# A scrap iota on GpSimd behind every second gather of a sorted graph-attention kernel

## The chip, the cores and the metric

The kernel runs on one core of one Trainium2 chip. The metric is the device time of one execution in microseconds (us), as the median of the runs shown. Durations inside the kernel come from one further execution that the hardware profiler recorded.

## The reference, cut to what matters

One layer of graph attention over 12,500 nodes of 64 features and 400,000 edges of 64 features. The edges come sorted by destination. Cut to what is computed:

```
h_src, h_dst = x[src], x[dst]
e     = leaky_relu(concat(h_src, h_dst, edge) @ W_attn + b_attn)      # one number per edge
alpha = softmax of e over the edges with the same dst
z     = segment_sum(alpha * (concat(h_src, edge) @ W_ne), dst)
out   = layernorm(x + relu(concat(x, z) @ W_out))
```

## The kernel before

**Tiling.** 512 consecutive edges are a group: 128 partitions by 4 places. There are 782 groups. The first 88 are worked off by one-hot matrix products, woven into the rest, and need no gather. The other 694 are the main part. They go in 45 batches, 41 of them of 16 groups and four smaller ones at the end; a batch is cut into tiles of up to four groups.

**Gathers.** For each group and place, GpSimd (POOL in the profile) issues one indirect DMA that fetches the source nodes' rows of 128 edges into a tile `zx` (`gather`, line 303; the DMA is line 314). A full tile takes 16 gathers, a batch of 16 groups takes 64. The first batch ("plain", 64 gathers) reads `x`. The later ones read `table`, in DRAM, in which each row of `x` has its score in front: 2,712 gathers. `zx` comes from the pool `feats` with eight buffers (`ZB = 8`), so gathers run up to two batches ahead of the products that read them, and a gather into a buffer waits until the products of the tile that held it before are done.

```
zx = feats.tile([P, SG, T, EW + D], F32, name="zx")
for g in range(n):
    for t in range(T):
        ...
        nc.gpsimd.indirect_dma_start(out=..., in_=table[:, :], in_offset=...)
```

**What a batch does.** `scores` copies the edges' features into `zx` on ScalarE (ACT, line 346) and makes the scores on VectorE (DVE, lines 348 to 366; line 355 is the first that needs the gathered rows). `softmax` runs over the whole batch in five stages that go from DVE to ACT to TensorE (PE) and back, with the work on the first 88 groups woven between the stages. Then `weights` (line 761), and `products` (line 775): 16 matmuls a tile, which read `zx` last and so set its buffer free. The products of a batch's first two tiles follow its softmax at once (`NOW = 2`). Those of the other two are put into `later`, and are done between the stages of the next batch's softmax. `add_in` (line 792) adds the products into the running sums `acc`; a block of nodes whose sums are complete is finished and written out.

**Order.** PE, DVE, ACT and SP run in the order in which the main loop is written (`manual_schedule`). GpSimd is not in that list: in the main loop its instructions are put in order by the framework's scheduler, which goes by its own estimate of times. Edge features, index lists and other plain loads are DMAs issued by SP.

**Front.** Ahead of the main loop, a front part loads `x`, makes the two scores of each node, writes `table`, and fetches windows of destination scores by seven indirect DMAs (`window`). It is written out by hand for all engines, POOL too. Behind it come a transpose, three small matmuls and three copies (lines 926 to 936) that make two products of the weights, `both` and `edge_both`, for which the scheduler finds a place.

Of the kernel before, what the change touches and what calls it, by code (L numbers as in the profile page):

```python
# [9 lines left out]
F32 = mybir.dt.float32  # L10
I32 = mybir.dt.int32
# [4 lines left out]
P = 128  # L16
# [13 lines left out]
SG = 4  # L30
# [18 lines left out]
NBC = 4  # L49
LATE = 8.0  # L50
NOW = 2

BF16 = mybir.dt.bfloat16
I16 = mybir.dt.int16
# [3 lines left out]
def sorted_path(ctx, tc, x, dst, idx, edge, w_ne, w_attn, b_attn, w_out, out, flag):  # L58
# [6 lines left out]
    nc = tc.nc  # L65
    N, D = x.shape
# [4 lines left out]
    NG = idx.shape[0]  # L71
# [5 lines left out]
    const = ctx.enter_context(tc.tile_pool(name="const", bufs=1))  # L77
# [3 lines left out]
    ident = const.tile([P, P], F32, name="ident")  # L81
# [51 lines left out]
    for i in range(2):  # L133
        nc.vector.memset(d3s[i], N)
    nc.vector.memset(mrow, FLOOR)
    nc.vector.memset(srow, 0.0)
    b_col = const.tile([P, 1], F32, name="b_col")
    wne = const.tile([P, D], F32, name="wne")
    wout = const.tile([D, 2, D], F32, name="wout")
    acc = const.tile([P, RING + S], F32, name="acc")  # L140
    xall = const.tile([P, NB, EW], F32, name="xall")

# [13 lines left out]
    both = const.tile([P, D], F32, name="both")  # L156
    twice = const.tile([P, P], F32, name="twice")
# [5 lines left out]
                   allow_small_or_imprecise_dtypes=True)  # L163
    places = const.tile([P, NB * NOD], I16, name="places")
    nc.gpsimd.iota(places, pattern=[[1, NB * NOD]], base=0, channel_multiplier=0,
                   allow_small_or_imprecise_dtypes=True)
# [16 lines left out]
    nc.vector.tensor_reduce(own, ident.rearrange("p (h n) -> p h n", n=ND), axis=AX.X, op=OP.add)  # L183
    node = const.tile([P, ND], F32, name="node")
    nc.vector.tensor_reduce(node, ident.rearrange("p (h n) -> p n h", n=ND), axis=AX.X, op=OP.add)
    meet = const.tile([1, 2], I32, name="meet")
    of_next = const.tile([1, 4], F32, name="of_next")
    scrap_row = const.tile([1, 1], F32, name="scrap_row")

    loop = ExitStack()  # L190
    chunks = loop.enter_context(tc.tile_pool(name="chunks", bufs=2))
# [115 lines left out]
    def gather(g0, n, srcs, b0, plain):  # L307
# [4 lines that stand above are left out]
                r = RP if g0 + g == NG - 1 else P  # L312
                at = srcs[0:r, g0 + g - b0, t:t + 1]
                nc.gpsimd.indirect_dma_start(  # L314
                    out=zx[0:r, g, t, 1:EW] if plain else zx[0:r, g, t, 0:EW], out_offset=None,
                    in_=x[:, :] if plain else table[:, :],
                    in_offset=bass.IndirectOffsetOnAxis(ap=at, axis=0))
        return zx

    fetched, early = {}, {}  # L320
# [479 lines left out]
                   allow_small_or_imprecise_dtypes=True)  # L800
    attn = pre.tile([P, 3 * D], F32, name="attn", bufs=1)
    nc.scalar.dma_start(out=attn, in_=w_attn.rearrange("k o -> o k").to_broadcast([P, 3 * D]))
    nc.scalar.dma_start(out=b_col, in_=b_attn.unsqueeze(0).to_broadcast([P, 1]))
    nc.scalar.dma_start(out=wne, in_=w_ne)
    nc.scalar.dma_start(out=wout, in_=w_out.rearrange("(h k) o -> k h o", h=2))
    lists = {0: listed(0)}
    xts = []
    for c0 in range(0, NB, CB):
# [15 lines left out]
    nc.sync.dma_start(out=meet, in_=dst[DG * GE - 1:DG * GE + 1].unsqueeze(0))  # L824
    sd = pre.tile([P, NB], F32, name="sd", bufs=1)
    NW = len(wins)
    d0p = const.tile([P, NW], I32, name="d0p")
    wks = [counts.rearrange("p h n -> p (h n)")[:, k * S:(k + 1) * S] for k in range(NW)]
    nc.scalar.activation(w_dst, attn[:, D:2 * D], AF.Copy)
    nc.scalar.activation(w_src, attn[:, 0:D], AF.Copy)  # L830
# [3 lines left out]
    with before:  # L834
# [23 lines left out]
        with tc.manual_schedule(engines={EngineType.DVE, EngineType.Pool, EngineType.Activation, EngineType.PE, EngineType.SP}):  # L858
            lots0 = [(g0, SG) for g0 in range(DG, DG + sizes[0], SG)]
            ahead = [gather(g0, n, lists[0], DG, True) for g0, n in lots0[:2]]  # L860
            for c0 in range(0, NB, CB):
                dots(c0, min(c0 + CB, NB), w_dst, sd[:, c0:min(c0 + CB, NB)])
            nc.vector.tensor_scalar(sd, sd, b_col, None, op0=OP.add)
            psd = psum.tile([P, SG, P], F32, name="pg", bufs=4)[0:NB, 0, :]
            nc.tensor.transpose(psd, sd, ident)
            sdt = pre.tile([NB, P], F32, name="sdt", bufs=1)
            nc.vector.tensor_copy(sdt, psd)
            nc.scalar.dma_start(out=sdflat[0:NB * P].rearrange("(b p) -> b p", p=P), in_=sdt)
            neighbours(0)
            for g0, n in lots0[:3]:  # L870
                early[g0] = edges(g0, n)
            for c0 in range(0, NB, 2 * CB):
                c1 = min(c0 + 2 * CB, NB)
                dots(c0, c1, w_src, xall[:, c0:c1, 0])
                nc.sync.dma_start(
                    out=table[c0 * P:c1 * P, :].rearrange("(b p) f -> p b f", p=P),
                    in_=xall[:, c0:c1, :])
            d0f = pre.tile([1, NG], F32, name="d0f", bufs=1)
            nc.vector.tensor_copy(d0f, d0i)
            for g0 in range(0, NG, 3 * P):  # L880
                n = min(3 * P, NG - g0)
                pb = psum.tile([P, SG, P], F32, name="pg", bufs=4).rearrange("p k n -> p (k n)")
                nc.tensor.matmul(pb[:, :n], ones_row, d0f[:, g0:g0 + n], start=True, stop=True)
                nc.scalar.activation(d0b[:, g0:g0 + n], pb[:, :n], AF.Copy)
            nc.vector.tensor_scalar(dn, d0f[:, 0:DG + 1], float(DN - 1), None, op0=OP.min)
            relf = pre.tile([1, DG], F32, name="relf", bufs=1)
            at = 0
            for n, many in CHUNKS:
                chunked = [a.rearrange("o (c g) -> o c g", g=n) for a in (relf[:, at:at + n * many], d0f[:, at:at + n * many])]
                nc.vector.tensor_tensor(chunked[0], chunked[1], chunked[1][:, :, 0:1].to_broadcast([1, many, n]), op=OP.subtract)  # L890
                at += n * many
            room = pre.tile([1, DG], F32, name="room", bufs=1)
            for a, b in spans:
                nc.vector.memset(room[:, a:b], float(ND - nodes_of(a)))
            over_ = pre.tile([1, DG], F32, name="over_", bufs=1)
            nc.vector.tensor_tensor(over_, relf, room, op=OP.subtract)
            nc.vector.tensor_reduce(fars[0:1, NK + len(spans):NK + len(spans) + 1], over_, axis=AX.X, op=OP.max)
            nc.vector.tensor_tensor(relf, relf, room, op=OP.min)
            nc.vector.tensor_scalar(rel, relf, 0.0, None, op0=OP.max)
            nc.vector.tensor_scalar(d0i, d0i, RING - 1, None, op0=OP.bitwise_and)  # L900
            window(0)
            ahead += [gather(g0, n, lists[0], DG, True) for g0, n in lots0[2:]]
            for k in range(1, NW):
                window(k)
            nc.scalar.activation(s_src, xall[:, :, 0], AF.Copy)
            nc.scalar.activation(count_, places[:, 0:P], AF.Copy)
            parted_row = pre.tile([DG, P, T], I32, name="parted_row", bufs=1)
            nc.vector.tensor_scalar(parted_row, ids[:, :, 0:T], P - 1, None, op0=OP.bitwise_and)
            low_row = pre.tile([DG, P, T], BF16, name="low_row", bufs=1)
            nc.scalar.activation(low_row, parted_row, AF.Copy)  # L910
            nc.sync.dma_start(out=low_rows, in_=low_row)
            of_dense = dense_list()
            dense_places(of_dense, fit)
            nc.vector.tensor_copy(of_next[:, 2:4], meet)
            nc.vector.tensor_tensor(of_next[:, 2:3], of_next[:, 2:3], of_next[:, 3:4], op=OP.is_equal)
            for c, (a, b) in enumerate(((starts[1], DG), (DG, begins[-2]))):
                nc.vector.tensor_tensor(earlies[:, NK + c:NK + c + 1], d0b[:, a:a + 1], d0b[:, b:b + 1], op=OP.subtract)
                nc.vector.tensor_scalar(earlies[:, NK + c:NK + c + 1], earlies[:, NK + c:NK + c + 1], -0.5, None, op0=OP.add)
            nc.vector.tensor_scalar(earlies[:, NK + 2:NK + 3], d0b[:, DG:DG + 1], -1.0, float(DN - 1), op0=OP.mult, op1=OP.add)
# [2 lines left out]
    rows = loop.enter_context(tc.tile_pool(name="rows", bufs=1))  # L922
    with tc.issue_after(last_of_front):
        nc.vector.memset(acc, 0.0)

    pwt = psum.tile([P, SG, P], F32, name="pg", bufs=4)
    nc.tensor.transpose(pwt[0:D, 0, :], wne, ident)
    for h in range(2):
        nc.scalar.dma_start(out=twice[h * D:(h + 1) * D, h * D:(h + 1) * D], in_=w_out[0:D, :])
    wt = work.tile([P, NBC // 2, P], F32, name="xtt", bufs=2)[0:D]  # L930
    nc.vector.tensor_copy(wt[:, 0, :], pwt[0:D, 0, :])
    nc.tensor.matmul(pwt[:, 1, 0:D], wt[:, 0, :], wout[:, 1, :], start=True, stop=True)
    nc.vector.tensor_copy(both, pwt[:, 1, 0:D])
    for g in range(2):
        nc.tensor.matmul(pwt[g * D:(g + 1) * D, 2, 0:D], wt[:, 0, D:P], wout[:, 1, :], start=True, stop=True)
    nc.vector.tensor_copy(edge_both, pwt[:, 2, 0:D])

    def late_of(k):

# [113 lines left out]
    k = 0  # L1053
# [703 lines left out]
```

## Time and profile before

| | before |
|---|---|
| median of 3 runs | 4319.42 us (4318.68 to 4326.91) |
| the profiled execution: time, span | 4329.98 us, 4328.3 us |
| granted TensorE clock, mean | 0.627 |
| busy: POOL, PE, DVE, ACT | 2637.9, 2048.5, 2000.6, 1048.5 us |
| gathers from `table` | 2712 of 947 ns |
| first and last start of these | 100.5 us, 4267.0 us |

Busy time is the time in which an engine works on some instruction; issuing instructions, semaphores and waits do not count. A row of a group reads: line, engine, operation, tiles, count, then busy time, mean duration in ns, idle time of that engine just before these instructions, and what ended most of that idle time ("issue" where the profile shows nothing that was waited for). A row of the timeline reads: start, duration, engine, line, operation, and in brackets the idle time before it with what ended it.

### The profile page before, as it was taken

Reading aid. Unit: us, or ns where it says so; the run is one execution under the profiler, and the core shown is the slowest. Engines: PE = TensorE matmul, PEld = TensorE weight load, DVE = VectorE, ACT = ScalarE, POOL = GpSimd, SP = SyncE. Lnnn points to the kernel's source line nnn. Section 1 sums busy time; section 2 is a strip of 40 time slices with the busy share of each in tenths; the row PEclk is TensorE's granted clock in tenths of the full one; section 3 lists DMA queues with packets and bytes.
Section 4 is the critical chain, followed back from the end, with each engine's and each line's share of the span. In section 5 each row is a group of like instructions: output and inputs, shape, how many; then the busy total and the mean of one; then the engine's idle time right before and its main releaser. Section 6 shows DMA issues by size and latency. Waiting matters only on the chain. (4 is left out here: it accounts for less than half of the span.)

```text
span 4328.3 us, 33932 instructions
## 1 busy us (share of the span) xinstructions
PE 2048.5 (47%) x8733; PEld 1795.4 (41%) x8733; DVE 2000.6 (46%) x5102; ACT 1048.5 (24%) x2333; POOL 2637.9 (61%) x2800
## 2 busy tenths in 40 slices
PE   0143334444554554554555455456455555443443
PEld 0143334444544444444444445444344433343433
DVE  4433434544445545444444445455444444444545
ACT  0111113222222323222223322233222223111112
POOL 6666666666666666656556565655555656666662
PEclk9999996555555555555565555556556555555555
DMA  9322223332322323232222222222222212322221
GB/s 115 63 58 51 53 59 66 61 65 47 66 56 56 69 51 76 50 68 56 56 55 57 57 57 56 52 61 64 37 51 47 60 36 51 71 37 47 53 55 27
DMA packets 490797, 246.18 MB, mean 57 GB/s; under 512 B 326795, under 2 KB 446154, under 8 KB 490594
## 3 DMA queue, kind: packets, MB, share of 16 engines
q1 hardware_dynamic: 398334, 150.93, 15.0%
q0 software_dynamic: 89056, 92.60, 13.9%
q8 instruction: 72, 1.18, 0.1%
q14 instruction: 131, 1.07, 0.1%
q10 hardware_dynamic: 3204, 0.39, 0.1%
HBM read 236.93 MB, written 6.75 MB: 56 GB/s over the span
## 5 line engine op out<-in xcount | busy, mean ns | idle before, releaser
L314 POOL DMA_INDIRECT zx<-table,srcs x2712 | 2568.2, 947 | 1599.5 <-issue 1199.5
L775 PE MATMUL pg<-w,zx 128*128 128x20 f32 (+9 forms) x5408 | 1113.9, 366 | 772.5 <-issue 689.6
L775 PEld LDWEIGHTS pg<-w,zx 128*128 128x128 f32 x5408 | 1140.3, 314 | 760.3 <-issue 686.6
L462 PE MATMUL pg<-big,lows 128*128 128x490 f32 (+3 forms) x704 | 398.3, 739 | 360.4 <-DVE lows L457 155.3
L462 PEld LDWEIGHTS pg<-big,lows 128*128 128x128 f32 x704 | 210.1, 315 | 495.1 <-issue 319.9
L568 PE MATMUL lines<-ident,bnd 128*1 128x128 f32 x180 | 52.8, 394 | 715.4 <-issue 487.1
L348 DVE TENSOR_TENSOR pr<-ze,fixed 128x1024 f32<-128x1024 f32 (+2 forms) x180 | 212.5, 1180 | 288.5 <-ACT fixed L345 164.6
L479 DVE TENSOR_TENSOR counts<-counts,pg 128x490 f32 (+3 forms) x88 | 48.0, 545 | 600.5 <-remote 461.9
L568 PEld LDWEIGHTS lines<-ident,bnd 128*1 128x1 f32 x180 | 12.1, 92 | 739.9 <-issue 502.3
L792 DVE TENSOR_TENSOR acc<-acc,pg 128x16 f32 (+9 forms) x694 | 128.5, 185 | 278.3 <-PE pg L775 147.5
L454 ACT ACTIVATE big<-places,place 128x490 f32<-128x490 int16 (+3 forms) x352 | 205.5, 584 | 205.5 <-remote 197.4
L350 DVE TENSOR_REDUCE fixed<-pr 128x16 f32<-128x1024 f32 (+2 forms) x180 | 214.1, 1189 | 24.8 <-DVE pr L348 10.1
L537 PE MATMUL pg<-xall,counts 128*128 128x256 f32 (+1 forms) x350 | 127.2, 490 | 161.6 <-issue 160.5
L415 PE MATMUL pg<-s_src,big 128*128 128x98 f32 x704 | 188.7, 446 | 1.3 <-issue 1.3
L346 ACT ACTIVATE zx<-ze 128x1024 f32<-128x1024 f32 (+2 forms) x180 | 185.2, 1029 | 8.7 <-issue 1.8
L345 ACT ACTIVATE fixed<-wrow 128x80 f32<-128x80 f32 (+9 forms) x180 | 47.0, 261 | 564.8 <-issue 289.7
L455 ACT ACTIVATE big<-big 128x490 f32<-128x490 f32 (+3 forms) x352 | 178.1, 506 | 11.2
L442 DVE TENSOR_TENSOR pr<-pr,pg 128x392 f32<-128x392 f32 x88 | 49.5, 563 | 278.6 <-remote 152.1
L415 PEld LDWEIGHTS pg<-s_src,big 128*128 128x128 f32 x704 | 172.8, 330 | 5.4 <-issue 5.2
L575 ACT ACTIVATE line<-tops 1x256 f32<-1x256 f32 x45 | 29.6, 658 | 575.3 <-DVE tops L677 424.4
L537 PEld LDWEIGHTS pg<-xall,counts 128*128 128x128 f32 (+1 forms) x350 | 84.4, 246 | 202.2 <-issue 191.7
L357 DVE TENSOR_TENSOR hot<-fixed,drel 128x320 bf16<-128x320 f32 (+9 forms) x180 | 112.1, 623 | 36.9 <-DVE fixed L355 22.8
(278 smaller groups left out, 2331.8 us busy)
## 6 DMA issues: line engine op xcount, KB each, us to landing
ze<-in_edge_dram SPq DMA_DIRECT2D x164, 512.0 KB
zx<-table,srcs POOLq DMA_INDIRECT x2712
low_of<-low_rows SPq DMA_DIRECT2D x88, 128.0 KB
ep<-in_edge_dram SPq DMA_DIRECT2D x88, 128.0 KB
ed<-in_edge_dram SPq DMA_DIRECT2D x29, 384.0 KB
table<-xall SPq DMA_DIRECT2D x7, 455.0 KB
ze<-in_edge_dram SPq DMA_DIRECT2D x8, 384.0 KB
out_dram<-yo SPq DMA_DIRECT2D x23, 128.0 KB
```

The costliest lines, as they stand in the source:

```text
L314: nc.gpsimd.indirect_dma_start(out=zx[0:r, g, t, 1:EW] if plain else zx[0:r, g, t, 0:EW], out_offset=None, in_=x[:, :] if plain else table ...
L346: nc.scalar.activation(zx[0:r, 0:n, :, EW:EW + D], ze[0:r, 0:n], AF.Copy)
L348: nc.vector.tensor_tensor(pr[0:r, 0:n], ze[0:r, 0:n], w_edge[0:r].unsqueeze(1).to_broadcast([r, n, T, D]), op=OP.mult)
L350: nc.vector.tensor_reduce(ysum[0:r, 0:n], pr[0:r, 0:n], axis=AX.X, op=OP.add)
L357: nc.vector.tensor_tensor(hot[0:r, 0:n], slots[0:r, 0:Sk].unsqueeze(1).unsqueeze(1).to_broadcast([r, n, T, Sk]), drel[0:r, :, b:b + n].rea ...
L415: nc.tensor.matmul(found[:, t, :], hot[:, :, t], s_src, start=True, stop=True)
L454: nc.scalar.activation(hi, places[:, 0:wide], AF.Square, bias=place[:, t, g:g + 1])
L455: nc.scalar.activation(hi, hi, AF.Relu, scale=-1.0, bias=1.0)
L462: nc.tensor.matmul(to, lows[t], highs[t], start=(t == 0), stop=(t == T - 1))
L537: nc.tensor.matmul(pairs[0:m * ND, 0:m * D], counts[:, h0:h0 + m, :].rearrange("l h n -> l (h n)"), xall[:, h0:h0 + m, 1:EW], start=(h0 == ...
L775: nc.tensor.matmul(pg[:, g, :], zx[:, g, t, 1:EW + D], w[:, g, t, :], start=(t == 0), stop=(t == T - 1))
L792: nc.vector.tensor_tensor(ag, ag, pg[:, g, :], op=OP.add)
```

## The change

Behind the gather of every second place (`t` odd) GpSimd gets an iota that writes a scrap tile of 128 x 300 numbers in 16 bits, `paused`, which nothing reads. This holds for gathers from `table` in all groups but the last: 677 groups with two iotas each, 1,354 iotas. The scrap tile needs room, so some small tiles (`b_col`, `wne`, `wout`, `meet`, `d0p`) move to a pool that the front part gives back, and the weight products `both` and `edge_both` are made inside the front, with their DMAs ahead of it.

```diff
+PAUSE = 300
...
+    paused = const.tile([P, PAUSE], I16, name="paused")
...
                     in_offset=bass.IndirectOffsetOnAxis(ap=at, axis=0))
+                if not plain and t % 2 and g0 + g + 1 < NG:
+                    nc.gpsimd.iota(paused, pattern=[[1, PAUSE]], base=0, channel_multiplier=0,
+                                   allow_small_or_imprecise_dtypes=True)
...
+    wout = pre.tile([D, D], F32, name="wout", bufs=1)
+    nc.scalar.dma_start(out=wout, in_=w_out[D:2 * D, :])
+    for h in range(2):
+        nc.scalar.dma_start(out=twice[h * D:(h + 1) * D, h * D:(h + 1) * D], in_=w_out[0:D, :])
...
(in the front, between the writing of the table and d0f:)
+            pwt = psum.tile([P, SG, P], F32, name="pg", bufs=4)
+            nc.tensor.transpose(pwt[0:D, 0, :], wne, ident)
+            wt = pre.tile([D, P], F32, name="wt", bufs=1)
+            nc.vector.tensor_copy(wt, pwt[0:D, 0, :])
+            nc.tensor.matmul(pwt[:, 1, 0:D], wt, wout, start=True, stop=True)
+            nc.vector.tensor_copy(both, pwt[:, 1, 0:D])
...
(the same steps, and the DMAs of twice, go out behind the front)
```

**Where the iotas stand in the built program.** The scheduler does not keep an iota behind its gather: an iota waits for nothing but the iota before it, on the one tile that they all write, while a gather waits for its buffer. In the built program the 1,354 iotas stand on POOL's queue in 45 lots, two of them (13 and 20) ahead of the first gather from `table`, all others within the first 1,184 gathers from it. The remaining 1,528 gathers have none. A stretch of POOL's queue, with the semaphore that each instruction waits for left out except on the iotas:

```
gathers x32
Iota paused 128x300 [each waits for the iota before]  x50      ahead of gather 480
gathers x16
Iota paused 128x300                                   x1       ahead of gather 496
gathers x16
Iota paused 128x300                                   x22      ahead of gather 512
gathers x32
Iota paused 128x300                                   x50      ahead of gather 544
...
Iota paused 128x300                                   x66      ahead of gather 1184
gathers x1528
```

Gathers are counted from 0 at the first one from `table`. Lots of one or two iotas, as the one ahead of gather 496, occur eleven times. Between gathers 96 and 288 the gathers stand in three runs of 64 with one lot between two runs.

More of the change, by code (lines that the diff above doesn't have):

```diff
@@ L136, in sorted_path @@
     nc.vector.memset(srow, 0.0)
-    b_col = const.tile([P, 1], F32, name="b_col")
-    wne = const.tile([P, D], F32, name="wne")
-    wout = const.tile([D, 2, D], F32, name="wout")
     acc = const.tile([P, RING + S], F32, name="acc")
@@ L185, in sorted_path @@
     nc.vector.tensor_reduce(node, ident.rearrange("p (h n) -> p n h", n=ND), axis=AX.X, op=OP.add)
-    meet = const.tile([1, 2], I32, name="meet")
     of_next = const.tile([1, 4], F32, name="of_next")
     scrap_row = const.tile([1, 1], F32, name="scrap_row")
+    paused = const.tile([P, PAUSE], I16, name="paused")
     loop = ExitStack()
@@ L802, in sorted_path @@
     nc.scalar.dma_start(out=attn, in_=w_attn.rearrange("k o -> o k").to_broadcast([P, 3 * D]))
+    b_col = pre.tile([P, 1], F32, name="b_col", bufs=1)
+    wne = pre.tile([P, D], F32, name="wne", bufs=1)
+    wout = pre.tile([D, D], F32, name="wout", bufs=1)
+    meet = pre.tile([1, 2], I32, name="meet", bufs=1)
     nc.scalar.dma_start(out=b_col, in_=b_attn.unsqueeze(0).to_broadcast([P, 1]))
     nc.scalar.dma_start(out=wne, in_=w_ne)
-    nc.scalar.dma_start(out=wout, in_=w_out.rearrange("(h k) o -> k h o", h=2))
+    nc.scalar.dma_start(out=wout, in_=w_out[D:2 * D, :])
+    for h in range(2):
+        nc.scalar.dma_start(out=twice[h * D:(h + 1) * D, h * D:(h + 1) * D], in_=w_out[0:D, :])
     lists = {0: listed(0)}
@@ L826, in sorted_path @@
     NW = len(wins)
-    d0p = const.tile([P, NW], I32, name="d0p")
+    d0p = pre.tile([P, NW], I32, name="d0p", bufs=1)
     wks = [counts.rearrange("p h n -> p (h n)")[:, k * S:(k + 1) * S] for k in range(NW)]
@@ L877, in sorted_path @@
                     in_=xall[:, c0:c1, :])
+            pwt = psum.tile([P, SG, P], F32, name="pg", bufs=4)
[4 more added lines that the diff above has]
+            nc.vector.tensor_copy(both, pwt[:, 1, 0:D])
+            for g in range(2):
+                nc.tensor.matmul(pwt[g * D:(g + 1) * D, 2, 0:D], wt[:, D:P], wout, start=True, stop=True)
+            nc.vector.tensor_copy(edge_both, pwt[:, 2, 0:D])
             d0f = pre.tile([1, NG], F32, name="d0f", bufs=1)
@@ L924, in sorted_path @@
         nc.vector.memset(acc, 0.0)
[L926 to L936, printed above, removed]
     def late_of(k):
```

## The prediction

> **What bounds the kernel now.** I read the page first, for the busy shares and the costliest groups.
>
> ```profile
> span 4328.3 us, 33932 instructions
> PE 2048.5 (47%) x8733; PEld 1795.4 (41%) x8733; DVE 2000.6 (46%) x5102; ACT 1048.5 (24%) x2333; POOL 2637.9 (61%) x2800
> L314 POOL DMA_INDIRECT zx<-table,srcs x2712 | 2568.2, 947 | 1599.5 <-issue 1199.5
> ```
>
> No engine is busy throughout; POOL is the busiest, nearly all of it gathers. Its idle time is of two kinds, which the timeline of POOL separates. These are the starts of the gathers around a few places: the first two from `table`, three tile borders, and the last gather that has iotas ahead of it in the new order.
>
> ```profile
> 100.52 0.95 POOL L314 DMA_INDIRECT zx<-table,srcs  x1 [0.30 <-issue]
> 101.77 0.94 POOL L314 DMA_INDIRECT zx<-table,srcs  x1 [0.30 <-issue]
> ...
> 282.36 0.94 POOL L314 DMA_INDIRECT zx<-table,srcs  x1 [0.30 <-issue]
> 290.06 0.95 POOL L314 DMA_INDIRECT zx<-table,srcs  x1 [6.76 <-issue]
> ...
> 820.05 0.95 POOL L314 DMA_INDIRECT zx<-table,srcs  x1 [0.30 <-issue]
> 824.78 0.95 POOL L314 DMA_INDIRECT zx<-table,srcs  x1 [3.79 <-ACT big L454]
> ...
> 843.55 0.95 POOL L314 DMA_INDIRECT zx<-table,srcs  x1 [0.30 <-issue]
> 848.59 0.95 POOL L314 DMA_INDIRECT zx<-table,srcs  x1 [4.09 <-issue]
> ...
> 887.35 0.95 POOL L314 DMA_INDIRECT zx<-table,srcs  x1 [0.30 <-issue]
> 895.22 0.95 POOL L314 DMA_INDIRECT zx<-table,srcs  x1 [6.92 <-issue]
> ...
> 1842.92 0.94 POOL L314 DMA_INDIRECT zx<-table,srcs  x1 [0.30 <-issue]
> 1864.77 0.94 POOL L314 DMA_INDIRECT zx<-table,srcs  x1 [20.91 <-issue]
> ```
>
> Between neighbours 0.30 us always passes, so a gather costs POOL 1.25 us from start to start, and 0.30 us is no wait. The longer gaps stand at tile borders: there the gather waits for its buffer. Split at the gather with number 1184 (the one at 1864.77), the view of windows gives the rest (a stretch and its length, busy time of PE, PE's weight loads, DVE, ACT and POOL, each with its count, then granted clock, DMA share and GB/s).
>
> ```profile
> 100.50:1864.80 1764.30, 796.23 (x3461) 752.07 (x3459) 785.64 (x2097) 407.33 (x963) 1123.11 (x1185) 0.69 0.30 59
> 1864.80:4268.00 2403.20, 1221.61 (x4920) 1018.68 (x4919) 1129.70 (x2774) 616.98 (x1306) 1445.12 (x1528) 0.57 0.26 54
> ```
>
> First part: 1,184 gathers of 1.25 us are 1480 us of 1764, so POOL waits 284 us there, 16%. Second part: 1,528 of them are 1910 of 2403, so it waits 493 us. Does the other side wait for the gathers? The view of the gather's line says who waited for it:
>
> ```profile
>   PE pg L775: 74.1, 33
>   PEld pg L775: 65.2, 32
>   POOL zx L314: 16.7, 41
>   PE lines L568: 15.3, 1
>   DVE fixed L355: 0.3, 2
> ```
>
> Hardly anyone: line 355, the first to need the rows, waited 0.3 us in all. What holds the buffers is seen in PE's timeline beside the gathers from 848.59 to 887.35:
>
> ```profile
> 869.11 5.35 PE L775 MATMUL pg<-w,zx 128*128 128x16 f32 x25
> 876.28 0.18 PE L775 MATMUL pg<-w,zx 128*128 128x16 f32 x1 [1.82 <-issue]
> 879.11 0.19 PE L775 MATMUL pg<-w,zx 128*128 128x16 f32 x1 [2.65 <-issue]
> ...
> 892.40 0.19 PE L775 MATMUL pg<-w,zx 128*128 128x16 f32 x1 [2.61 <-issue]
> 893.85 2.17 PE L415 MATMUL pg<-s_src,big 128*128 128x98 f32 x8 [1.26 <-issue]
> 896.25 3.60 PE L775 MATMUL pg<-w,zx 128*128 128x16 f32 x16
> ```
>
> 25 matmuls take 5.35 us, then single ones come 2 to 2.8 us apart with nothing that they wait for, and full pace is back at 893.85, 5.5 us after the last gather of the run ended (887.35 + 0.95). The gather at 895.22 follows on that. So a long run of gathers goes with slow stretches on PE, which hold the buffers, for which POOL then waits. POOL, with 84% of its time taken by gathers, and this loop share the bound.
>
> **The iotas.** POOL works its queue in order. The built program has the iotas in lots at tile borders, all 1,354 ahead of gather 1184: 33 ahead of the first, 1,321 among the next 1,184. What one costs is bounded by the start of the same timeline and the groups kept apart by shape.
>
> ```profile
> 0.81 0.20 POOL masks.py:197 MEMSET ident<- 128x128 f32 x1 [0.29 <-POOLq L1745]
> 1.06 0.13 POOL L162 IOTA p_col<- 128x1 f32 x1
> 1.16 0.28 POOL masks.py:199 TENSOR_SCALAR_AFFINE_SELECT ident<-ident 128x128 f32<-128x128 f32 x1
> 1.41 0.54 POOL L165 IOTA places<- 128x490 int16 x1
> 1.91 0.17 POOL L799 IOTA slots<- 128x48 f32 x1
> ```
>
> ```profile
> L165 POOL IOTA places<- 128x490 int16 x1 | 0.5, 537 | 0.0
> L799 POOL IOTA slots<- 128x48 f32 x1 | 0.2, 175 | 0.0
> ```
>
> Two iotas give (537 - 175) / 442 = 0.82 ns a column, so 300 columns last 175 + 252 x 0.82 = 0.381 us. From start to start the one of 490 columns takes 1.91 - 1.41 = 0.50 us; less 190 columns that is 0.344 us, for an iota that waits for nothing. Here each waits for the end of the one before. The only row with such a wait is the select on `ident`: it starts at 1.16, the memset that it waits for ends at 1.01, so a wait adds 0.15 us at most. Low end 0.344; high end 0.381 + 0.15 = 0.53; I take 0.45, near the middle of 0.38 and 0.53, as the wait is certain and its cost is only bounded. The lots then last 1,354 x 0.45 = 609 us (467 to 718).
>
> The Trainium skill has a rule on this: its page "Perfetto Trace Analysis" (the section on the per-instruction lifecycle, GPSIMD Engine Instruction) says to time GpSimd by the start-to-start spacing of consecutive instructions, as reported spans are unreliable. By it the price would be 0.344 and the whole change +183 us, the low end below; the rows for that spacing are of iotas without a wait. Its "GPSIMD Engine Reference" (section 2.1, Instruction dispatch) says that an instruction completes only when all eight of its cores are done and the data has landed, which no row here shows by itself; it speaks for the part above 0.344, against this change.
>
> **What hides them.** Part of the lots falls into waits. Ahead of gather 544 (the one at 895.22) stand 50 iotas, 22.5 us, where POOL waited 6.6 us; ahead of gather 512 (848.59) 22, 9.9 us, against 3.8. As all waits of the first part are only 284 us, POOL can't reach gather 1184 sooner than 1480 + 609 us of work allow: 609 - 284 = 325 us later than now (183 to 434). This is the path: POOL, in order, and each gather behind a lot waits for all of it.
>
> Do waits remain beside the lots? With 9.9 and 22.5 us free of gathers in each batch, the slow stretches (which end 5.5 us after a run) leave PE, DVE and ACT some 20 us of full pace ahead of each run of two tiles, so the products should free the buffers while the lots run. Uncovered are eleven places with one or two iotas, such as 824.78, 3.5 us each, and three without any, such as 290.06, 6.5 us each: 57 us if all stay. I count them as gone, and put 57 on the high end.
>
> **The second part** has no iotas and the order of before. The other engines come into it with all their work done, so at most the wait at its start goes once, 20.9 us; the loop then returns to its waits. 21 us go on the low end, none into the forecast. Behind the last gather nothing changes.
>
> ```profile
> 4267.05 0.87 POOL L314 DMA_INDIRECT zx<-table,srcs  x1 [0.30 <-issue]
> ```
>
> From there to the span's end are 61 us, as before.
>
> **The front.** The weight products move ahead of `d0f` on DVE and PE: three copies and three matmuls with a few turns between the engines.
>
> ```profile
> 93.13 0.27 DVE L931 COPY xtt<-pg 64x128 f32<-64x128 f32 x1
> ...
> 95.89 0.22 DVE L933 COPY both<-pg 128x64 f32<-128x64 f32 x1
> ```
>
> Even if both stretches of 2.8 us between copies stay, that is under 6 us on DVE, while POOL goes through 64 gathers from `x`, seven windows and now 33 iotas, 15 us which are in the 609. In the first part POOL sets the pace, so this costs nothing; without that cover, 6 us.
>
> **Sum.** The profiled execution took 4329.98 us with a span of 4328.3, 10.6 above the median of 4319.42, so the differences from it are put on the median: 4319 + 325 = 4644 us. The forecast's own range is 4319 + 183 - 21 = 4481 to 4319 + 434 + 57 = 4810.
>
> **Rivals.**
>
> *The waits stay beside the lots.* If what frees a buffer comes later by as much as POOL does, lots and waits add up: 4319 + 609 = 4928 us (4786 to 5037). For it: PE's slow stretches go with the gathers, and two runs of 16 now stand as one of 32. Against it: line 355 hardly ever waited for a gather, so those engines don't start from POOL's end alone. 16%.
>
> *Faster: the gathers are paced.* Two gathers and an iota take 2.95 us. Were the iotas worked off one behind every second gather, as the source reads, all gathers would start 1,354 x 2.95 us = 3994 us after 100.5, at 4095 instead of 4267; if the runs were then thin enough that slow stretches and waits vanish, the time would be 4150. It decides for faster if under 170 of today's 284 + 493 us of waits stay. Against it: the built order has the lots, and with them runs of 32 and 64 gathers stay; with this order, faster needs iotas below 284 / 1354 = 0.21 us. 4%.
>
> *Cheap iotas.* At 0.25 us, below both ways of reading the rows, the lots take 338 us: 4319 + 54 = 4373. 5%. At 0.21 us they just fill the waits and nothing changes: 1%.
>
> **How the numbers follow.** Forecast 74%, rivals 16, 4, 5 and 1%. A measurement here can tell some 0.2% from no change (9 us; the runs lie 8 apart). Slower by more: 74 + 16 + 5 = 95%; faster 4%, the same 1%. The range starts at the forecast's low end, 4480, and goes into the first rival, to 4860, which leaves out the half of that rival and the last three, about 19%.
>
> **What would show it.** After the change: 1,354 iotas of about 0.38 us on POOL, 0.4 to 0.53 us from start to start, in lots; gather 1184 starts near 2190 us instead of 1865; hardly an idle gap over 1 us on POOL before that; behind it the old pattern, some 2400 us to the last gather. I am wrong if iotas stand singly between gathers, if they start under 0.3 us apart, if gaps of several us stand beside the lots, or if the second part takes much less than 2400 us.

## The result, and the profile after

The changed kernel takes 4680.58 us (median of 4 runs, 4676.44 to 4685.95) against 4323.16 us before (4318.68 to 4329.57) on the same chip: a ratio of 1.0826, with a 95% interval of 1.0805 to 1.0848. That is 357 us slower. The profiled execution took 4676.44 us, 346.5 more than that of before.

The page after: span, busy times, and the groups of the gather, of PE's products, of the iota and of line 356 (line 355 before).

```profile
span 4674.7 us, 35277 instructions
PE 2037.8 (44%) x8733; PEld 1784.9 (38%) x8733; DVE 1999.8 (43%) x5102; ACT 1046.5 (22%) x2333; POOL 3140.6 (67%) x4154
L312 POOL DMA_INDIRECT zx<-table,srcs x2712 | 2559.2, 944 | 1350.0 <-issue 1175.6
L776 PE MATMUL pg<-w,zx 128*128 128x20 f32 (+9 forms) x5408 | 1106.6, 367 | 641.3 <-issue 573.3
L317 POOL IOTA paused<- 128x300 int16 x1354 | 511.6, 378 | 94.9 <-POOL paused L317 6.2
L356 DVE TENSOR_TENSOR fixed<-fixed,zx 128x16 f32<-128x16 f32 (+2 forms) x180 | 33.1, 184 | 239.8 <-DMA zx<-table,srcs 232.4
```

POOL is busy 503 us longer, all of it iotas; the gathers are what they were. Line 356, which hardly waited for gathers before, now waits 232 us for them: POOL is late for the others.

The view of windows, split as before at gather 1184:

```profile
114.05:2212.60 2098.55, 816.02 (x3614) 767.61 (x3614) 807.47 (x2172) 423.83 (x1001) 1616.41 (x2506) 0.69 0.25 51
2212.60:4614.60 2402.00, 1190.99 (x4764) 992.53 (x4764) 1101.17 (x2692) 596.40 (x1263) 1441.85 (x1528) 0.56 0.26 53
```

Gather 1184 starts 347.8 us later (2212.60 against 1864.77); the second part is as long as before (2402.0 against 2403.2). POOL's timeline shows the lots and what is left of the waits:

```profile
409.76 0.94 POOL L312 DMA_INDIRECT zx<-table,srcs  x1 [0.30 <-issue]
416.99 0.94 POOL L312 DMA_INDIRECT zx<-table,srcs  x1 [6.29 <-issue]
...
541.99 0.94 POOL L312 DMA_INDIRECT zx<-table,srcs  x1 [8.91 <-issue]
...
926.88 0.94 POOL L312 DMA_INDIRECT zx<-table,srcs  x1 [0.30 <-issue]
927.83 0.39 POOL L317 IOTA paused<- 128x300 int16 x1
928.38 0.94 POOL L312 DMA_INDIRECT zx<-table,srcs  x1 [0.16 <-issue]
...
2181.90 0.94 POOL L312 DMA_INDIRECT zx<-table,srcs  x1 [0.30 <-issue]
2182.85 29.34 POOL L317 IOTA paused<- 128x300 int16 x66
2212.60 0.94 POOL L312 DMA_INDIRECT zx<-table,srcs  x1 [0.40 <-PE pg L416]
```

66 iotas go by in 29.34 us, 0.445 us each, and the gather behind them starts at once. Three gaps of several us stand at borders without a lot: 6.3 us at gather 192 (416.99), 8.9 at gather 272 (541.99) and 8.6 at gather 336. At gather 192 POOL waited before the change too (6.7 us); at the other two it did not (0.30). Each of the three stands 32 or 48 gathers behind the last lot of more than one iota. In all, gaps over 1 us up to gather 1184 hold 29 us in 8 places, beyond the usual 0.30; before it was 280 us in 48.

### The profile page after: what moved, and what is told of

Same layout as the page of the kernel before. It is cut to its first block, busy times and chain, and to the rows that moved or that the text cites. A ratio compares the mean times of both kernels' runs of the same rounds, so it can differ in the third digit from the quotient of the medians.

```text
span 4674.7 us, 35277 instructions
## 1 busy us (share of the span) xinstructions
PE 2037.8 (44%) x8733; PEld 1784.9 (38%) x8733; DVE 1999.8 (43%) x5102; ACT 1046.5 (22%) x2333; POOL 3140.6 (67%) x4154
## 3 DMA queue, kind: packets, MB, share of 16 engines
q0 software_dynamic: 89056, 92.60, 12.8%
## 5 line engine op out<-in xcount | busy, mean ns | idle before, releaser
L317 POOL IOTA paused<- 128x300 int16 x1354 | 511.6, 378 | 94.9 <-POOL paused L317 6.2
L356 DVE TENSOR_TENSOR fixed<-fixed,zx 128x16 f32<-128x16 f32 (+2 forms) x180 | 33.1, 184 | 239.8 <-DMA zx<-table,srcs 232.4
```

What stands on the lines that cost most here:

```text
L317: nc.gpsimd.iota(paused, pattern=[[1, PAUSE]], base=0, channel_multiplier=0, allow_small_or_imprecise_dtypes=True)
```

## The experiments

The same program takes different times on different chips. The runs below were made on four chips: on the first three the kernel before took 3551, 3544 and 3543 us, on the last 4344 us, near the 4323 us of the result. These are called kind B (about 3545) and kind A (about 4320 to 4345, the chip of the result among them). Each run is set against the kernel before on its own chip. Only the kernel before and the changed kernel were run on both kinds, and of the kernel before there is a trace on kind A alone; on kind B the run without iotas stands in for it. Each chip was met in one sitting, so these runs can't tell a lasting property of a chip from a condition that it was in at the time; "kind" names the group, not its cause. Runs 1, 2, 3 and 6 shared the first chip, 4, 5 and 7 the second, 8, 9 and the repeat of 6 the third, 10 and 11 the last.

**1. The edits without the iotas.**

```diff
-                if not plain and t % 2 and g0 + g + 1 < NG:
-                    nc.gpsimd.iota(paused, pattern=[[1, PAUSE]], base=0, channel_multiplier=0,
-                                   allow_small_or_imprecise_dtypes=True)
```

> The changed kernel with its iotas left out; all the other edits of the change stay (the small tiles in the front's pool, the weight products made inside the front). Theory (POOL's queue): the whole of the slowdown comes from the iotas, so this is the kernel before again: 4320 us, within 10 either way, gather 1184 starts within 10 us of 1865. Rival (the moved front or the moved tiles cost something): the first gather from the table stays near 114 us as in the changed kernel instead of 100, and the time is 4330 or more.

Measured: 3551.18 us against 3551.16 us, ratio 1.0001 (0.9991 to 1.0010). The moved tiles and the moved front cost nothing here, so the slowdown is the iotas. The times themselves are 770 us lower than expected. First the group of PE's products on the page of before, then the page of this run, and the windows of its two parts:

```profile
L775 PE MATMUL pg<-w,zx 128*128 128x20 f32 (+9 forms) x5408 | 1113.9, 366 | 772.5 <-issue 689.6
```

```profile
span 3543.3 us, 33923 instructions
L312 POOL DMA_INDIRECT zx<-table,srcs x2712 | 2562.3, 945 | 826.5 <-issue 766.8
L773 PE MATMUL pg<-w,zx 128*128 128x20 f32 (+9 forms) x5408 | 1095.1, 375 | 10.9 <-DVE w L759 10.6
L353 DVE TENSOR_TENSOR fixed<-fixed,zx 128x16 f32<-128x16 f32 (+2 forms) x180 | 33.1, 184 | 679.2 <-DMA zx<-table,srcs 675.9
```

```profile
101.48:1582.82 1481.34, 799.75 (x3543) 741.81 (x3544) 800.63 (x2156) 415.46 (x987) 1120.48 (x1184) 0.70 0.35 71
1582.82:3490.10 1907.28, 1112.47 (x4905) 946.38 (x4906) 1118.95 (x2739) 605.36 (x1287) 1441.84 (x1528) 0.59 0.33 67
```

The gathers last as long (945 ns), but PE's products idle 10.9 us instead of 772.5: the 689.6 us of "issue" are gone, and with them the slow stretches (PE's rows in which single matmuls start a few us apart, with nothing that the profile shows to wait for). POOL has no gap over 1 us; its 1,184 gathers of the first part take 1481 us, which is 1.25 us each and no wait. On a chip of kind B POOL alone is the bound, and DVE waits 676 us for it.

**2. and 3. Shorter iotas, in lots.**

```diff
-PAUSE = 300
+PAUSE = 150
```

> The iota writes 150 columns instead of 300, the number of iotas stays 1,354. The scheduler now puts them in 31 lots, the last ahead of gather 864 (which starts at 1374.6 us before, with 194 us of POOL's waits ahead of it). Theory (POOL's queue is a sum, and the waits ahead of the last lot hide what they can): an iota lasts 175 + 102 x 0.82 = 0.26 us and starts some 0.07 after the one before ends, 0.33 us each, 447 us together; less 194, plus some 20 of waits that stay: 4320 + 273 = 4593 us (4570 to 4620). Rival (the waits stay, lots and waits add up): 4320 + 447 = 4767. Rival (the cost goes with the length of the lots alone, whatever is hidden, so half the columns give half of the 357 us): 4500.

```diff
-PAUSE = 300
+PAUSE = 20
```

> The iota writes 20 columns instead of 300; still 1,354 of them, now in 16 lots, the last ahead of gather 544 (which starts at 895.2 us before, with 115 us of POOL's waits ahead of it). Theory (POOL's queue is a sum): 175 - 28 x 0.82 = 0.15 us and 0.07 of waiting, 0.22 us each, 298 us together; less 115, plus some 15 of waits that stay: 4320 + 198 = 4518 us (4480 to 4550). So the iota at the prediction's price of no change, 0.21 us, would still cost some 170 us, as the lots now end where POOL has waited for 115 us only, not 284. Rival (what counts is the price of an iota against 284 / 1354 = 0.21 us): 4320 to 4340. Rival (lots and waits add up): 4618.

Measured: 3988.15 us with 150 columns (ratio 1.1229, 1.1210 to 1.1248) and 3842.09 us with 20 (1.0816, 1.0798 to 1.0834). All the expected times missed, as they were made with the waits of kind A. The price per iota held. The groups, with 150 columns and with 20:

```profile
L317 POOL IOTA paused<- 128x150 int16 x1354 | 343.4, 254 | 90.5
```

```profile
L317 POOL IOTA paused<- 128x20 int16 x1354 | 197.4, 146 | 91.5
```

Busy and idle time together are 434 and 289 us, 0.320 and 0.213 us an iota, and the kernels are 437 and 291 us slower. With no wait to fill, the whole price shows. What a break-even price would be on a chip with waits, these two runs can't say.

**4. The changed kernel again.** No edit.

> The changed kernel once more. The first four experiments met a chip on which the kernel before takes 3551 us and POOL has no gap over 1 us between gathers; the result was measured where it takes 4320 us and POOL waits 777 us. Theory (the cost is the lots less what of POOL's waits they fill): where the kernel before takes about 3551 us there is nothing to fill, so all 1,354 x 0.445 = 603 us show: 4154 us (4140 to 4170). Where it takes about 4320 us: 4680 again. Rival (the cost is a share of the time, 8.3%): 3845. Rival (the same 357 us on either): 3908.

Measured: 4145.45 us against 3543.54, ratio 1.1698 (1.1678 to 1.1718), 602 us more. That is 1,354 x 0.445 = 603 and rules out both rivals. The same two kernels differ by 357 us on kind A, where POOL waits, and by 602 on kind B, where it doesn't. The groups of this run, and its windows:

```profile
L317 POOL IOTA paused<- 128x300 int16 x1354 | 513.4, 379 | 90.0
L356 DVE TENSOR_TENSOR fixed<-fixed,zx 128x16 f32<-128x16 f32 (+2 forms) x180 | 33.1, 184 | 1297.1 <-DMA zx<-table,srcs 1294.3
```

```profile
114.98:2189.20 2074.22, 825.30 (x3621) 760.74 (x3621) 810.00 (x2178) 427.29 (x1007) 1622.85 (x2505) 0.66 0.25 51
2189.20:4100.40 1911.20, 1086.12 (x4827) 925.07 (x4829) 1103.06 (x2703) 593.52 (x1260) 1445.50 (x1528) 0.59 0.33 66
```

Gather 1184 starts at 2189 us here and at 2213 on the chip of the result, though without iotas these were 1583 and 1865: with the lots in, POOL's own queue sets the time on both, and 24 us are left of a difference of 282. The iotas themselves cost the same on both (379 and 378 ns).

**5. What the wait for the iota before costs.** The iotas write two scrap tiles in turn.

```diff
-    paused = const.tile([P, PAUSE], I16, name="paused")
+    paused = [const.tile([P, PAUSE], I16, name=f"paused{k}") for k in range(2)]
...
-                    nc.gpsimd.iota(paused, pattern=...
+                    nc.gpsimd.iota(paused[t // 2], pattern=...
```

with PAUSE = 150.

> As with 150 columns, but the iotas write two scrap tiles in turn, so each waits for the one before the last instead of the last; lots and numbers of columns are the same. Theory (an iota that need not wait for the one before overlaps it, as the rows before showed for iotas without a wait: start to start 0.037 us less than the duration of 0.537): 0.22 us from start to start instead of 0.322, 298 us in all instead of 436; where the kernel before takes 3551 us, 3849 (3830 to 3880). Rival (the spacing has nothing to do with the wait; an iota holds POOL for 0.32 us): 3987, as with one tile.

Measured: 3819.16 us (ratio 1.0777, 1.0759 to 1.0795), 276 us more than before instead of 437. The scheduler made 18 lots of these iotas, not the 31 that were expected to stay, which does not matter where no wait is to be filled. A lot in the timeline, and the group:

```profile
901.06 28.33 POOL L317 IOTA paused<- 128x150 int16 x139
```

```profile
L317 POOL IOTA paused<- 128x150 int16 x1354 | 276.6, 274 | 0.1
```

28.33 us for 139 is 0.204 us from start to start, less than the 0.274 that each lasts: they overlap. So of the 0.320 us with one tile, 0.12 us, over a third, came of waiting for the iota before.

**6. and 7. One iota between gathers.** POOL joins the engines whose order is as written; then behind every fourth gather instead of every second.

```diff
-with tc.manual_schedule(engines={EngineType.PE, EngineType.DVE, EngineType.Activation, EngineType.SP}):
+with tc.manual_schedule(engines={EngineType.PE, EngineType.DVE, EngineType.Activation, EngineType.SP, EngineType.Pool}):
```

> The same iotas of 300 columns, with POOL added to the engines whose order is as written: one iota stands behind every second gather all the way, no lots. By the changed kernel's rows a gather is followed by an iota after 0.95 us and an iota by a gather after 0.55 to 0.81 us, so two gathers and an iota take 1.25 + 0.95 + 0.55 to 0.81 = 2.75 to 3.01 us, 1,354 of them 3724 to 4075 us; with the front (100) and the tail (61) no less than 3885 to 4236 us. Theory (the slow stretches of the other engines come of runs of gathers 1.25 us apart, and go where the gathers are thinner; they make most of POOL's 777 us of waits): most of the waits vanish, 4100 to 4250 us, faster than before. Rival (the waits come of the buffers and the batch's chain whatever the density): POOL's waits stay over 500 us and the time is 4500 us or more.

```diff
-                if not plain and t % 2 and g0 + g + 1 < NG:
+                if not plain and t == 3 and g0 + g + 1 < NG:
```

> Iotas of 300 columns, in the order as written, but only behind every fourth gather: 677 of them. Theory (POOL's queue is a sum, and a single iota between two gathers costs 0.26 us, as the kernel with one behind every second gather showed: 352.5 us / 1,354): where the kernel before takes 3551 us, 3551 + 677 x 0.26 = 3727 (3715 to 3740). Rival (a lone iota costs its 0.445 us as in a lot): 3852. Where the kernel before takes 4320 us, POOL's waits decide: four gathers and an iota take 5.26 us, 1.32 us a gather, under the 1.42 us a gather at which the other engines seemed to lose no ground, so the waits would stay in part: 4200 to 4450.

Measured: 3903.65 us for every second (ratio 1.0991, 1.0973 to 1.1009), 3717.15 for every fourth (1.0491, 1.0473 to 1.0508): 352.5 and 173.6 us more, 0.26 us an iota in both. The first run could not test its theory, as a chip of kind B has no slow stretches to cure. The second agreed with the sum (176). Run once more, the first gave the same, on kind B again:

> Eight buffers and one iota of 300 columns behind every second gather, in the order as written, once more. Where the kernel before takes 3551 us: 3904 again (353 more, 0.26 us an iota). Where it takes 4320 us and the other engines show slow stretches in runs of gathers: if these come of gathers 1.25 us apart, as on the chip of the result, they go, and the time is near 3904 as well, faster than 4320; if they do not depend on the spacing, POOL's waits stay over 500 us and it is 4500 or more.

Measured: 3895.33 us, ratio 1.0993 (1.0975 to 1.1012). Its timeline:

```profile
999.54 0.95 POOL L312 DMA_INDIRECT zx<-table,srcs  x1 [0.30 <-issue]
1000.50 0.39 POOL L317 IOTA paused<- 128x300 int16 x1
1001.06 0.94 POOL L312 DMA_INDIRECT zx<-table,srcs  x1 [0.16 <-issue]
1002.30 0.94 POOL L312 DMA_INDIRECT zx<-table,srcs  x1 [0.30 <-issue]
```

The iota starts as the gather ends, and the next gather 0.16 us behind the iota instead of 0.30 behind a gather. So 1001.06 - 999.54 = 1.52 us take the place of 1.25. A lone iota is cheaper than one in a lot (0.26 against 0.445).

**8. and 9. Six buffers, so that POOL waits on kind B too.** To test how waits hide lots where there are none, six buffers of gathered rows instead of eight, without and with the iotas. Without iotas the traces show the same order of POOL, PE, DVE and ACT as with eight buffers.

```diff
-ZB = 8
+ZB = 6
```

> The changed kernel without its iotas and with six buffers of gathered rows instead of eight (ZB = 6). The order of every engine is that of eight buffers; only what a gather waits for changes: the products of the tile six before. This is to bring back waits of POOL at tile borders on a chip that shows none with eight. Theory: the gather of a batch's first tile then waits for products that come between the stages of the batch before's softmax, so waits of some 5 to 20 us a batch appear, 200 to 850 us over 42 batches: 3750 to 4400 where the kernel before takes 3551. Rival (the buffers are free that early anyway): 3551, no gap over 1 us. Where the kernel before takes 4320, more than that: 4400 to 5000.

> The same six buffers with the 1,354 iotas of 300 columns, in 44 lots at tile borders, the last ahead of gather 1152. Theory (waits ahead of a gather that has a lot before it are filled by the lot): slower than the run without iotas by 603 us less POOL's waits there ahead of gather 1152, give or take 40; if these are 300 us, by about 300. Rival (lots and waits add up, as what frees the buffers comes later by as much as POOL does): slower by 603, with as much waiting left in the first part as without iotas.

Measured: 4145.12 us without (ratio to the kernel before 1.1699, 1.1679 to 1.1718) and 4497.01 with the iotas (1.2694, 1.2673 to 1.2715). Six buffers brought the waits back, some 14 us once a batch, as expected; and the iotas cost 352 us, not 603. The last border with a lot, and the one that answers to it, first without and then with iotas:

```profile
1782.24 0.95 POOL L312 DMA_INDIRECT zx<-table,srcs  x1 [0.30 <-issue]
1797.70 0.94 POOL L312 DMA_INDIRECT zx<-table,srcs  x1 [14.52 <-issue]
```

```profile
2130.78 0.94 POOL L312 DMA_INDIRECT zx<-table,srcs  x1 [0.30 <-issue]
2131.73 9.30 POOL L317 IOTA paused<- 128x300 int16 x21
2146.15 0.94 POOL L312 DMA_INDIRECT zx<-table,srcs  x1 [5.13 <-PE pg L776]
```

9.30 us of iotas and 5.13 us of waiting are 14.43 us, the 14.52 of before: the gather starts when its buffer is free, and the lot fits into the time until then. The windows ahead of this gather (number 1152) and behind it, without iotas and with them:

```profile
101.50:1797.70 1696.20, 792.92 (x3458) 733.41 (x3459) 784.44 (x2102) 404.07 (x962) 1091.67 (x1152) 0.70 0.30 61
1797.70:4107.60 2309.90, 1148.04 (x5042) 975.40 (x5042) 1141.32 (x2815) 623.71 (x1323) 1473.89 (x1560) 0.57 0.28 56
```

```profile
114.30:2146.15 2031.85, 801.78 (x3458) 742.15 (x3459) 777.28 (x2089) 401.68 (x955) 1585.68 (x2473) 0.68 0.25 51
2146.15:4453.80 2307.65, 1139.83 (x5042) 964.86 (x5042) 1141.24 (x2815) 623.64 (x1323) 1471.67 (x1560) 0.58 0.28 56
```

Without iotas POOL waits 1696 - 1152 x 1.25 = 256 us there. With them, the 5 us shown are the only gap over 1 us, so 603 - 256 + 5 = 352 us were due, and 352 came. The second parts are equal. Lots and waits do not add up.

**10. The same iotas in another place.** Six buffers, one iota behind every second gather (ZB = 6, and POOL in the order as written).

> Six buffers, with the same 1,354 iotas of 300 columns behind every second gather instead of in lots at the borders. With six buffers POOL waits once a batch, 14 us, ahead of a batch's first gather, for products that follow the softmax of the batch whose last gather went just before. Theory (a wait is filled only by iotas that stand between the last gather that the waited-for work needs and the gather that waits): iotas inside the batch put its last gather off, the wait starts later and is as long as before, so their 0.26 us each come on top: slower than six buffers without iotas by 352 us, 4497 (4470 to 4520), POOL's waits still near 615 us. Rival (any iota fills a wait, wherever it stands): the 352 us vanish in the 615, 4145 to 4200.

Measured: 4654.11 us where the kernel before took 4344.23 (ratio 1.0703, 1.0676 to 1.0731). This chip is of kind A, so the time can't be set against the 4145 or the 4497 us. What is left are the rows:

```profile
2003.69 0.39 POOL L317 IOTA paused<- 128x300 int16 x1
2018.18 0.94 POOL L312 DMA_INDIRECT zx<-table,srcs  x1 [14.10 <-issue]
```

At the same border, gather 1152, POOL still waits 14.1 us, with 32 iotas worked off inside the batch of 64 gathers just before. That agrees with the theory but does not show it: there is no run of six buffers without iotas on this chip, so neither the length of this wait without iotas nor what they cost is known here. In all, gaps over 1 us hold 760 us, where the run without iotas on kind B had 615. PE's slow stretches are still there. The first line is of this run, the second of experiment 11 on the same chip, which has eight buffers and gathers 1.25 and 1.27 us apart in turn:

```profile
L776 PE MATMUL pg<-w,zx 128*128 128x20 f32 (+9 forms) x5408 | 1140.6, 369 | 577.9 <-issue 542.0
```

```profile
L776 PE MATMUL pg<-w,zx 128*128 128x20 f32 (+9 forms) x5408 | 1116.4, 368 | 767.1 <-issue 712.8
```

With gathers 1.25 and 1.52 us apart in turn, 542 us of "issue" remain of 713. In the slow stretches most single products of experiment 11 start 2.1 or 2.8 us behind the one before; here half of them start 1.4 us behind. So where the gathers are thinner the slow stretches are milder, and not gone; as the number of buffers differs too, the spacing is not shown to be the cause. Whether one iota of 300 columns behind every second gather makes the kernel faster on such a chip with eight buffers, as the rival of the prediction and two expectations had it, was not run there.

**11. A short iota between gathers.** POOL in the order as written, PAUSE = 20, eight buffers.

> Eight buffers, iotas of 20 columns behind every second gather. Theory (behind a gather an iota starts as the gather ends, and fills part of the 0.30 us that pass between two gathers anyway): from an iota's start to the next gather 0.557 us with 300 columns, less 280 columns of 0.82 ns, is 0.33 us, so an iota costs 0.95 + 0.33 - 1.25 = 0.03 us, 41 us in all: 3585 (3560 to 3600) where the kernel before takes 3545. Rival (an iota has a least price of 0.21 us, as in a lot): 3833.

Measured, on the same chip: 4338.86 us against 4344.23, ratio 0.9982 (0.9966 to 0.9998), the runs of before lying between 4324 and 4354. Its rows:

```profile
1500.39 0.94 POOL L312 DMA_INDIRECT zx<-table,srcs  x1 [0.30 <-issue]
1501.34 0.16 POOL L317 IOTA paused<- 128x20 int16 x1
1501.65 0.94 POOL L312 DMA_INDIRECT zx<-table,srcs  x1 [0.16 <-issue]
```

From the gather ahead of the iota to the one behind it 1.26 us pass here (1.27 in the mean) instead of 1.25, so the short iota fits into the 0.30 us that pass between gathers anyway. At the rival's 0.21 us, POOL would have had 284 us more to do. It is the rows that decide this: the time alone would not, as POOL waits 735 us on this chip, which could hide some of it, and the expected times were for kind B. The 1,354 iotas are nearly free, and no gain worth having either: a fifth of a per cent, with the interval's end at 0.9998. As this kernel has the moved tiles and the moved front as well, they cost nothing that shows on kind A either. No experiment pointed to a version that is clearly faster than the kernel before.

## Why the prediction was right

*The bound.* It held on the chip of the result, and its two halves are separated now: POOL's 1.25 us a gather is the same in every run, while the slow stretches and POOL's waits of 777 us, which the prediction put down to them, are there on kind A and not on kind B. That fits its account; the prediction took them as the kernel's own. That POOL and the loop share the bound is right for kind A; on kind B POOL is the bound alone. "Hardly anyone" waits for the gathers passes over the 74.1 us of PE's products in the view that it read; these come behind line 355 of the same tile, which had waited 0.3 us for the same rows, so the conclusion stands.

*The price of an iota, 0.45 us (0.344 to 0.53).* Measured 0.445 in the lots, with a duration of 378 ns (381 was worked out). The slope of 0.82 ns a column from two rows is (0.445 - 0.213) / 280 = 0.83 in the lots. The wait, which the prediction bounded by 0.15 us on top of the duration, is 0.445 - 0.378 = 0.067 us. That 0.45 came so near is in part luck: the rows bounded the wait only, and the middle was taken.

The rule of the Trainium skill that was weighed (its page "Perfetto Trace Analysis", GPSIMD Engine Instruction: go by the start-to-start spacing, not by the reported span) agrees with experiment 5, 0.204 us of spacing against 0.274 of duration. The rule was sound, and the +183 us did not come because the rows that gave 0.344 were of iotas that wait for nothing; in experiment 5 the wait for the iota before made 0.12 us of the spacing.

*What hides them.* 284 us of waits were counted as gone. 29 us stayed: 23 of them at gathers 192, 272 and 336, where no lot stands, 3 behind a lot of six, and 3 in four gaps of 1 us inside lots. The waits at the eleven places with one or two iotas, which stood on the prediction's high end, are gone. Of the three borders that it listed there as uncovered, at gathers 128, 192 and 256, only the one at 192 kept its wait; the 8.9 and 8.6 us at 272 and 336 are new. So gaps of several us do stand beside the lots, which it named as a sign of being wrong, but few; that their sum stayed within its 57 us is partly luck, as two of the places were others.

So 603 - 284 + 29 = 348 us, against 347.8 at gather 1184. Against the profiled executions the forecast of 325 was 22 us short: 29 us of waits instead of 0, less 7 of the price. The other 15 of the 37 us between 4644 and 4681 lie between executions: the profiled one of before took 10.6 us more than the median on which the forecast stands, and that of after 4 less than its own. Experiments 8 and 9 show the mechanism under control: the lot fills the wait.

*The second part* with its old length, 2402 us, and *the front* at nothing (experiment 1) came as said. Gather 1184 was put near 2190 and started at 2213, which is the 29 us less the 7. Two roundings in the sums change nothing: 1,354 x 0.344 is 466 and not 467, and the chances left out of the range add up to 18% and not 19.

*The rivals.* "The waits stay beside the lots" (4928) is ruled out by the 29 us left and by experiments 8 and 9. "Faster: the gathers are paced" did not happen in the built order. Its 2.95 us for two gathers and an iota are 1.25 + 1.52 = 2.77 us as measured, as a lone iota costs less than one in a lot. On kind B paced iotas cost 352 us; on kind A, with eight buffers and 300 columns, it is open. "Cheap iotas": the price was above both figures; in a lot even 20 columns cost 0.213.

What the prediction could not see in one profile is that the credit of 255 us belongs to the kind of chip: on kind B the same change costs 602 us.

## What to carry to other kernels

An instruction added to the busiest engine's queue costs its start-to-start spacing, less the waits that it stands right in front of; so look up where the built program puts it, and count the waits there and nowhere else. In experiment 9 work put right ahead of a wait filled it. That work fills a wait only if what ends the wait does not depend on anything behind that work is an argument, with which experiment 10 agrees. Credit that rests on a wait is only as lasting as the cause of that wait: here it was worth 255 us on one chip and nothing on another.

## What the runs showed of the hardware

- The same program took 3543 to 3551 us on three chips, and 4319 to 4344 us on those of the result and of the last two experiments, with the gathers at 944 to 947 ns on both kinds. On kind A PE starts single products mostly 2 to 2.8 us apart during long runs of gathers, with nothing that the profile shows to wait for: 690 us of "issue" ahead of PE's products before the change, 573 after it; on kind B these products wait 10.9 us in all. POOL itself is not slowed. The granted clock does not set the kinds apart (the changed kernel had 0.632 on kind A and 0.635 on kind B), nor do the packets of the DMA queues: the profiles of the kernel before on kind A and of the run without iotas on kind B have the same 89,056 packets on queue q0, that of the gathers, and on the instruction queue q14 the same 131, busy 0.1% of the time. What differs between these chips, and why long runs of gathers bring it out, no run told.
- An iota that need not wait for the one before starts before that one has ended: 0.204 us apart at a duration of 0.274 (150 columns). With the wait, 0.320.
- Two gathers in a row leave 0.30 us between them; behind an iota the next gather starts after 0.16 us, so an iota of 20 columns between two gathers costs about 0.01 to 0.02 us and one of 300 columns 0.26.
